# Cross-attention on one core: the first weight halves, the context and two block transposes are turned in another order

## The chip, the cores and the metric

The kernel runs on one core of a Trainium2 chip. Its engines are TensorE (PE in the profile, PEld for its weight loads), VectorE (DVE), ScalarE (ACT), GpSimd (POOL) and SyncE (SP), which here only issues transfers. The metric is the time of one execution on the device in microseconds; a lower time is better. Three executions of the kernel before took 283.97, 283.01 and 283.19 us, so its median is 283.19 us.

## The reference

One cross-attention layer with eight heads of width 256. There are 16 batches of 256 queries (width 256) and 77 keys (width 192), all in float32. The mask of the inputs is all ones.

```python
Q = (img_embed @ Wq).reshape(B, -1, H, D).transpose(0, 2, 1, 3)
K = (sent_embed @ Wk).reshape(B, -1, H, D).transpose(0, 2, 1, 3)
V = (sent_embed @ Wv).reshape(B, -1, H, D).transpose(0, 2, 1, 3)
score = jnp.einsum('bhqd,bhkd->bhqk', Q, K) / math.sqrt(D)
mask = (atten_mask != 0)[:, None, None, :]
score = jnp.where(mask, score, -jnp.inf)
attn = jax.nn.softmax(score, axis=-1)
ctx = jnp.einsum('bhqk,bhkd->bqhd', attn, V).reshape(B, -1, H * D)
out = ctx @ Wo + img_embed
mu = jnp.mean(out, axis=-1, keepdims=True)
var = jnp.var(out, axis=-1, keepdims=True)
return (out - mu) * jax.lax.rsqrt(var + EPS) * gamma + beta
```

## The kernel before

**What it computes.** The kernel never forms Q and K. For each head it multiplies the two weight matrices with each other once, G = Wk Wqᵀ / 16, and then multiplies the context c by G for a group of four batches: a = c G. Scores are then x aᵀ. Because the width of Wk is 192, G is kept in two pieces: `gA` (128 rows) and `gB` (the last 64 rows, two heads to a tile). The context is likewise kept turned, as `cA` and `cB`. In the same way Wv and Wo of a head are joined to one matrix (`uA`, `uB`).

**The opening stage.** To multiply Wk by Wq on TensorE both have to be turned, so that the head's width lies on the partitions. Half of the heads is turned on TensorE: `turn_q`, `turn_k`, `turn_k_last` and `turn_c` (for the context) each run four or six transposes into one or two PSUM banks, and copies then take the result to SBUF. The helper `evacuate` gives these copies in turn to ScalarE (line 151) and VectorE (line 153). The other half of the heads is turned by VectorE alone: `turn_blk(e)` (line 640) runs two stream transposes on blocks that were loaded as `wk_blk` and `wq_blk`. `keep_busy(n)` runs n transposes of the identity, whose results nobody reads.

**Order of the work.** The program writes each engine's order out by hand (a manual schedule): each engine does its instructions in the order of the lines. All loads are issued on SP, in the order of lines 567 to 594. In the diff's stretch, lines 751 to 766, the order on TensorE is: the first half of Wk's first 128 rows (`turn_k(0)`), Wk's last 64 rows for both halves (`turn_k_last`), the first half of Wq (`turn_q(0, 0)` and `turn_q(0, 1)`), their product (`g_of(0)`, line 719), the second half of Wk and of Wq, their product, the products for the last 64 rows (`rest_of_g`, line 733), and the first four batches' context (`turn_c(0, first)`, where `first` is 3). After this comes `a_of_places((0, 1))`, called A below: 64 matmul records at line 199 with `gA` (part A), 64 at line 213 with `gB` (part B), then eight copies to SBUF. Its eight outputs fill all eight PSUM banks. After A come the products for the heads that VectorE turned: `of_pair` (line 676, tile `pgb`) and `rest_of_pairs` (line 690, tile `phb`), A for the other places, the rest of the context, Wv times Wo (tiles `pu` and `pw`), and `prepare_last` (tile `pr`).

**The steady part.** From 58 us on a loop over the batches runs scores, softmax, the product with the values and the normalisation. PSUM tiles of all stages share one ring of eight banks, so a tile can be written when the copy of the tile eight places earlier is done.

Of the kernel before, what the change touches and what calls it, by code (L numbers as in the profile page):

```python
# [17 lines left out]
D = 256  # L18
# [35 lines left out]
def kernel(  # L54
# [13 lines left out]
    nc = tc.nc  # L68
# [67 lines left out]
    def flat(ap):  # L136
        return ap.rearrange("p a b -> p (a b)")
# [10 lines left out]
    def evacuate(dst, src):  # L148
        evacs[0] += 1
        if evacs[0] % 2:  # L150
            nc.scalar.copy(dst, src)  # L151
        else:
            nc.vector.tensor_copy(dst, src)  # L153
# [388 lines left out]
    with tc.tile_pool(name="wonce", bufs=1) as wp:  # L542
# [5 lines left out]
        wk_last = wp.tile([P, 2 * D], F32, tag="wl", name="wk_last")  # L548
# [8 lines left out]
        wk_ends = wk[P:].rearrange("r (e f) -> (r e) f", e=2)  # L557
# [5 lines left out]
        def load_c(lo, hi):  # L563
            nc.sync.dma_start(c_sb[:, lo:hi, :], c_rows[:, lo:hi, :])

        first = -(-GB * S2 // CR)
        nc.sync.dma_start(wk_nat[:, 0], wk_rows[0][:, : 2 * D])
        nc.sync.dma_start(wk_last, wk_ends[:, : 2 * D])
        nc.sync.dma_start(wq_nat[:, 0], wq_rows[0][:, :, : 2 * D])
        nc.sync.dma_start(wk_nat[:, 1], wk_rows[1][:, : 2 * D])  # L570
        nc.sync.dma_start(wq_nat[:, 1], wq_rows[1][:, :, : 2 * D])
        load_c(0, first)
        for e in range(2):
            load_blocks(wk_blk[:, e], wk_blocks[2 * e + 1])
# [24 lines left out]
        def keep_busy(n):  # L599
            for i in range(n):  # L600
                nc.tensor.transpose(idle, ident, ident)
# [9 lines left out]
        def turn_chunks(of, name):  # L611

            pt = ps_mm.tile([P, 4, P], F32, tag="mm", name=f"pt_{name}")
            for i, chunk in enumerate(of):
                nc.tensor.transpose(pt[:, i], chunk, ident)
            return pt

        def turn_q(e, u):
            chunks = [
                wq_nat[:, e, t, u * D + dc * P : u * D + (dc + 1) * P]  # L620
                for dc in range(2) for t in range(2)
            ]
            pt = turn_chunks(chunks, f"q_{e}_{u}")
            evacuate(flat(qT[:, e, u]), flat(pt))

        def turn_k(e):
            pt = turn_chunks([wk_nat[:, e, n * P : (n + 1) * P] for n in range(4)], f"k_{e}")
            evacuate(
                kT[:, e].rearrange("p u n l -> p (u n) l")[:, :, :P], pt
            )  # L630

        def turn_k_last():
            pt = turn_chunks([wk_last[:, n * P : (n + 1) * P] for n in range(4)], "kl")
            for e in range(2):
                evacuate(
                    kT[:, e].rearrange("p u n l -> p (u n) l")[:, :, P:],
                    pt.rearrange("p n (r e) -> p e n r", e=2)[:, e],
                )

        def turn_blk(e):  # L640
            for blk, of in ((wk_blk, kT_blk), (wq_blk, qT_blk)):
                nc.vector.transpose(
                    of[:, e].rearrange("p n (m r) -> p m n r", r=BK),
                    blk[:, e].rearrange("p m (n c) -> p m n c", c=BK),
                )

        def turn_c(lo, hi):
            for r in range(lo, hi, 2):
                n = min(2, hi - r)
                pc = ps_mm.tile([P, 4, P], F32, tag="mm", name=f"pc_{r}")  # L650
                for lc in range(2):
                    for j in range(n):
                        nc.tensor.transpose(
                            pc[:, 2 * lc + j, :CR],
                            c_sb[:, r + j, lc * LB : lc * LB + P],
                            ident[:CR, :CR],
                        )
                rows = slice(r * CR, (r + n) * CR)
                evacuate(flat(cA)[:, rows].rearrange("p (j m) -> p j m", m=CR), pc[:, :n, :CR])
                evacuate(  # L660
                    flat(cB)[LB:, rows].rearrange("p (j m) -> p j m", m=CR),
                    pc[LB:, 2 : 2 + n, :CR],
                )
                nc.gpsimd.tensor_copy(flat(cB)[:LB, rows], flat(cB)[LB:, rows])  # L664
# [34 lines left out]
        def two_banks(name, j):  # L699
            return [ps_mm.tile([P, 2, DI], F32, tag="mm", name=f"{name}_{j}_{e}") for e in range(2)]  # L700
# [13 lines left out]
        def g_of(e):  # L714

            pg = ps_mm.tile([P, 2, DI], F32, tag="mm", name=f"pg_{e}")
            for u in range(2):
                for dc in range(2):
                    nc.tensor.matmul(  # L719
                        pg[:, u],  # L720
                        kT[:, e, u, dc, :P],
                        qT[:, e, u, dc],
                        start=(dc == 0),
                        stop=(dc == 1),
                    )
            nc.scalar.mul(gA[:, NF * e : NF * e + 2], pg, D ** -0.5)

        def rest_of_g(u):

            ph = ps_mm.tile([P, DI], F32, tag="mm", name=f"ph_{u}")  # L730
            for dc in range(2):
                for e in range(2):
                    nc.tensor.matmul(
                        ph[half(e)],
                        kT[:, e, u, dc, P:],
                        qT[:, e, u, dc],
                        start=(dc == 0),
                        stop=(dc == 1),
                    )
            nc.vector.tensor_scalar(gB[:, u], ph, D ** -0.5, None, ALU.mult)  # L740

        def a_of_places(places, between=None):
            part_A, part_B, copies = prepare_a(0, places)
            part_A()
            part_B()
            for i, (dst, src) in enumerate(copies()):
                evacuate(dst, src)
                if between and i == 3:
                    between()

        turn_k(0)
        keep_busy(2)
        turn_k_last()
        keep_busy(3)
        turn_q(0, 0)
        turn_q(0, 1)
        g_of(0)
        turn_k(1)
        turn_q(1, 0)
        turn_q(1, 1)  # L760
        g_of(1)
        rest_of_g(0)
        rest_of_g(1)
        turn_c(0, first)
        turn_blk(0)
        a_of_places((0, 1), lambda: turn_blk(1))
        pg = two_banks("pgb", 0)
        for e in range(2):
            of_pair(pg, e, wk_part, wq_part)
# [7 lines left out]
        nc.sync.dma_start(gam, gamma.partition_broadcast(P))  # L777
        nc.sync.dma_start(bet, beta.partition_broadcast(P))
        a_of_places((2, 3))
        turn_v(3)  # L780
        turn_c(first, NCR)
# [167 lines left out]
```

## Time and profile before

| What | Value |
|---|---|
| Median of three executions | 283.19 us (283.01 to 283.97) |
| The profiled execution's own time | 282.59 us |
| Its span, first to last instruction | 280.8 us |
| TensorE busy | 270.8 us, 96% of the span |
| VectorE, ScalarE, GpSimd busy | 206.1, 166.5, 168.2 us |
| Transfers | 22.61 MB, mean 81 GB/s |
| Start of A's matmuls (line 199) | 17.27 us |
| First scores of the loop (line 313) | 58.25 us |

The profiled execution took 1.8 us more than its span; that is what lies around the first and the last instruction. All times in the text count from the span's start. A weight load or a matmul in float32 appears as more than one record, and a matmul's end is modelled, so a start is the better mark of time on TensorE. The time from a transfer's issue to its landing isn't that of the bytes alone: transfers queue behind each other.

### The profile page before, as it was taken

The numbers are of one execution on the slowest core, as the hardware profiler recorded it, in microseconds if no ns is written. First come the engines' busy times: TensorE is split into PE (matmuls) and PEld (weight loads), VectorE is DVE, ScalarE is ACT, GpSimd is POOL, SyncE is SP. The second block draws the span as 40 slices with busy tenths as digits, with TensorE's granted clock in tenths as the row PEclk, the third lists the DMA queues.
The fourth block names the chain that finished last, engine by engine and source line by source line (L and its number), as shares of the span: only waits on it lengthen the run. The fifth ranks groups of instructions, "written<-read, shape, count | busy, mean of one in ns | idle before, by whom it ended". The sixth has DMA issues, their size and how long they took to land.

```text
span 280.8 us, 13274 instructions
## 1 busy us (share of the span) xinstructions
PE 270.8 (96%) x5925; PEld 195.6 (70%) x5925; DVE 206.1 (73%) x421; ACT 166.5 (59%) x447; POOL 168.2 (60%) x228
## 2 busy tenths in 40 slices
PE   7899999999999999999999999999999999999990
PEld 7756589985586868686868686868686868476550
DVE  0255762668748989888889787777797978788873
ACT  2312142148547767676767676767686866968751
POOL 1000049955677777786867878777778445426173
PEclk9999999999999999999999999999999999999996
DMA  6998898940000010960100109501001011010112
GB/s 191 246 230 176 279 267 227 166 139 4 2 6 2 5 40 2 191 189 5 42 3 5 40 5 198 180 8 38 7 2 42 2 42 38 4 41 2 40 37 78
DMA packets 35641, 22.61 MB, mean 81 GB/s; under 512 B 17712, under 2 KB 34048, under 8 KB 35584
## 3 DMA queue, kind: packets, MB, share of 16 engines
q1 hardware_dynamic: 35584, 21.77, 30.8%
q8 instruction: 46, 0.75, 1.2%
q14 instruction: 11, 0.09, 0.1%
HBM read 17.57 MB, written 4.19 MB: 77 GB/s over the span
## 4 chain that ended last, share of the span: by engine, by line
PE 89%; POOL 2%; ACT 2%; DMA 2%; DVE 2%; issue 0%; SPq 0%; ACTq 0%; POOLq 0%
PE ps L313 23%; PE pa L199 12%; PE pv L241 9%; PE po L429 9%; PE pm L429 7%; PE pa L213 6%; PE pv L252 5%; PE po L378 5%; PE pu L676 3%; PE pr L274 2%; DMA wq_nat<-in_L_xattn_Wq_dram 2%; ACT e L342 1%; PE pg L719 1%; PE pgb L676 1%; PE pw L690 1%; PE pr L284 1%
## 5 line engine op out<-in xcount | busy, mean ns | idle before, releaser
L342 ACT ACTIVATE e<-s,top 128x77 f32<-128x77 f32 x256 | 67.1, 346 | 52.1 <-DVE top L335 49.9
L356 POOL TENSOR_TENSOR p<-e,rden 128x512 f32<-128x512 f32 x64 | 45.8, 738 | 46.6 <-DVE rden L350 46.4
L313 PE MATMUL ps<-a,xT 128*32 128x154 f32 x2048 | 70.0, 294 | 0.0
L313 PEld LDWEIGHTS ps<-a,xT 128*32 128x32 f32 x2048 | 66.2, 110 | 1.6 <-issue 0.7
L328 DVE TENSOR_TENSOR s<-ps,bias 128x308 f32<-128x308 f32 x64 | 30.3, 475 | 17.6 <-PE ps L313 15.9
L199 PE MATMUL pa<-cA,gA 128*32 128x308 f32 x512 | 35.8, 423 | 0.4 <-ACT cA L151 0.4
L462 POOL TENSOR_TENSOR xg<-xg,m 128x256 f32<-128x256 f32 x33 | 24.2, 733 | 13.5 <-DVE xg L476 11.8
L199 PEld LDWEIGHTS pa<-cA,gA 128*32 128x32 f32 x512 | 16.4, 110 | 21.1 <-issue 7.6
L241 PE MATMUL pv<-uA,cA 128*32 128x512 f32 x256 | 30.4, 592 | 0.0
L366 DVE STREAM_TRANSPOSE pT<-p 128x640 f32<-128x640 f32 x32 | 25.6, 824 | 2.4 <-POOL p L356 2.4
L348 DVE TENSOR_REDUCE den<-e 128x8 f32<-128x616 f32 x32 | 24.7, 772 | 3.5 <-ACT e L342 3.5
L335 DVE TENSOR_REDUCE top<-s 128x8 f32<-128x616 f32 x32 | 25.4, 795 | 1.1
L664 POOL COPY cB<-cB 64x224 f32<-64x224 f32 (+1 forms) x6 | 1.9, 358 | 36.8 <-DVE cB L153 36.8
L392 POOL TENSOR_TENSOR ts<-vw 128x768 f32<-128x768 f32 x11 | 22.0, 1997 | 0.0
L213 PE MATMUL pa<-cB,gB 64*32 64x308 f32 x512 | 19.5, 420 | 0.0
L378 PE MATMUL po<-vw,pT 128*32 128x256 f32 x320 | 19.2, 380 | 0.0
L861 ACT COPY vw<-pv 128x512 f32<-128x512 f32 x32 | 16.9, 578 | 2.5 <-PE pv L252 2.5
L495 ACT ACT_TABLE_LOAD x14 | 18.0, 1283 | 0.3
L213 PEld LDWEIGHTS pa<-cB,gB 64*32 64x32 f32 x512 | 9.7, 107 | 11.3 <-issue 7.6
L252 PE MATMUL pv<-uB,cB 64*32 64x512 f32 x256 | 17.4, 601 | 0.0
L524 DVE SCALAR_TENSOR_TENSOR xg<-xg,mv,gam 128x256 f32<-128x256 f32 x25 | 17.1, 682 | 0.0
L861 ACT COPY a<-pa 128x308 f32<-128x308 f32 x48 | 16.6, 446 | 0.0
(114 smaller groups left out, 440.1 us busy)
## 6 DMA issues: line engine op xcount, KB each, us to landing
xT<-in_x_dram SPq DMA_DIRECT2D x16, 256.0 KB, 6.4
xg<-in_x_dram SPq DMA_DIRECT2D x4, 1024.0 KB, 8.0
out_dram<-xg SPq DMA_DIRECT2D x15, 256.0 KB, 2.3
wo<-in_L_xattn_Wo_dram SPq DMA_DIRECT2D x4, 512.0 KB, 5.3
wvT<-in_L_xattn_Wv_dram SPq DMA_DIRECT2D x16, 96.0 KB, 3.7
wq_nat<-in_L_xattn_Wq_dram SPq DMA_DIRECT2D x2, 512.0 KB, 6.7
wq_blk<-in_L_xattn_Wq_dram SPq DMA_DIRECT2D x8, 128.0 KB, 4.3
wk_blk<-in_L_xattn_Wk_dram SPq DMA_DIRECT2D x8, 96.0 KB, 6.1
```

The source lines that it names most:

```text
L199: nc.tensor.matmul(flat(o[i * BK : (i + 1) * BK]), gA[:, h, cols(dc, i)], flat(cA[:, batches, :]), start=not B_first, stop=B_first,)
L213: nc.tensor.matmul(flat(banks[j + k][i * BK : (i + 1) * BK]), gB[half(k), h % NF, cols(dc, i)], flat(cB[half(k), batches, :]), start=B_fir ...
L241: nc.tensor.matmul(pv[k][i * BK : (i + 1) * BK], cA[:, b, k * BK : (k + 1) * BK], uA[:, parts, :, i], start=True, stop=False,)
L252: nc.tensor.matmul(pv[k][i * BK : (i + 1) * BK], cB[half(k), b, k * BK : (k + 1) * BK], uB[half(k), parts, :, i], start=False, stop=True,)
L313: nc.tensor.matmul(ps[m // 2][i * BK : (i + 1) * BK, m % 2 * 2 * S2 : (m % 2 + 1) * 2 * S2], xT_of[g][:, j * NM + m, dc], flat(a_of[g][:, ...
L328: nc.vector.tensor_tensor(s[:, a * H // 2 : (a + 1) * H // 2], ps[a][:, : H // 2 * S2].rearrange("p (h k) -> p h k", k=S2), bias[:, b, :]. ...
L342: nc.scalar.activation(e[:, h], s[:, h], AF.Exp, bias=top[:, h : h + 1])
L356: nc.gpsimd.tensor_tensor(part, e_mh[:, :, :, keys], rden_mh.unsqueeze(3).to_broadcast(list(part.shape)), ALU.mult,)
L366: nc.vector.transpose(pT_of[t].rearrange("p n m q -> p m n q"), p.rearrange("p m (n k) -> p m n k", k=BK),)
L378: nc.tensor.matmul(po[i * BK : (i + 1) * BK], pT[:, n, i], vw_of[b][:, 2 - n // 2 * 2 : 4 - n // 2 * 2, n % 2, :] if n < NF else vr[:, b, ...
L429: nc.tensor.matmul(out[i * BK : (i + 1) * BK], weight[:, i], moving, start=(n == 0), stop=(n == len(terms) - 1),)
L861: nc.scalar.copy(dst, src)
```

## The change

Four things move; no arithmetic is added or taken out, apart from one transpose of `keep_busy`.

- SP issues the load of Wk's last 64 rows (`wk_last`) after both halves of Wq and the second half of Wk, no longer ahead of them.
- `turn_k_last` moves behind `turn_q(1, 1)`, and the two `keep_busy` calls (2 and 3) become one of 4.
- `turn_k(1)` moves ahead of `g_of(0)`, and `turn_c(0, first)` moves ahead of `g_of(1)`.
- `turn_blk(1)`, which ran on VectorE after A's first four copies, moves ahead of A.

```diff
         nc.sync.dma_start(wk_nat[:, 0], wk_rows[0][:, : 2 * D])
-        nc.sync.dma_start(wk_last, wk_ends[:, : 2 * D])
         nc.sync.dma_start(wq_nat[:, 0], wq_rows[0][:, :, : 2 * D])
         nc.sync.dma_start(wk_nat[:, 1], wk_rows[1][:, : 2 * D])
         nc.sync.dma_start(wq_nat[:, 1], wq_rows[1][:, :, : 2 * D])
+        nc.sync.dma_start(wk_last, wk_ends[:, : 2 * D])
         load_c(0, first)
...
-        def a_of_places(places, between=None):
+        def a_of_places(places):
             part_A, part_B, copies = prepare_a(0, places)
             part_A()
             part_B()
-            for i, (dst, src) in enumerate(copies()):
+            for dst, src in copies():
                 evacuate(dst, src)
-                if between and i == 3:
-                    between()

         turn_k(0)
-        keep_busy(2)
-        turn_k_last()
-        keep_busy(3)
+        keep_busy(4)
         turn_q(0, 0)
         turn_q(0, 1)
+        turn_k(1)
         g_of(0)
-        turn_k(1)
         turn_q(1, 0)
         turn_q(1, 1)
+        turn_k_last()
+        turn_c(0, first)
         g_of(1)
         rest_of_g(0)
         rest_of_g(1)
-        turn_c(0, first)
         turn_blk(0)
-        a_of_places((0, 1), lambda: turn_blk(1))
+        turn_blk(1)
+        a_of_places((0, 1))
```

## The prediction

> **What bounds the kernel now.** I read the page's busy shares and chain first, to see whether an early gain can reach the end at all.
>
> ```profile
> PE 270.8 (96%) x5925; PEld 195.6 (70%) x5925; DVE 206.1 (73%) x421; ACT 166.5 (59%) x447; POOL 168.2 (60%) x228
> ...
> PE 89%; POOL 2%; ACT 2%; DMA 2%; DVE 2%; issue 0%; SPq 0%; ACTq 0%; POOLq 0%
> ```
>
> TensorE carries 89% of the chain. The DMA share (2%, the page names wq_nat) is one wait at the start; POOL's and most of ACT's and DVE's shares are the last 20 us. So whatever makes A start earlier moves the rest with it, unless a later transfer or copy is then too late. Next, the chain in order of time (start, duration, what):
>
> ```profile
> 1.62 5.56 DMA wq_nat<-in_L_xattn_Wq_dram
> 7.18 0.04 issue
> 7.23 0.67 PE pt_q L615 x4
> ...
> 7.92 0.70 DVE qT L153
> ...
> 8.76 1.97 PE pg L719 x8
> 10.72 0.44 PE pt_k L615 x4
> 11.16 0.45 PE pt_q L615 x4
> ...
> 11.63 0.59 ACT qT L151
> ...
> 12.27 1.99 PE pg L719 x8
> 14.27 1.88 PE ph L733 x16
> 16.14 0.55 PE pc L653 x4
> ...
> 17.27 4.35 PE pa L199 x64
> ```
>
> TensorE waits for the first half of Wq until 7.18, then three times for a copy: before the first pg, before the second, and before A. From 17.27 to 58 each piece of the chain is TensorE's. The third view is SP's issues in order of time, for the transfers:
>
> ```profile
> 3.08 0.47 SPq L564 DMA_DIRECT2D c_sb<-in_ctx_dram  x1
> ...
> 11.74 0.31 SPq L561 DMA_DIRECT2D wq_blk<-in_L_xattn_Wq_dram  x1
> ```
>
> The answers by tile give issue to landing: wk_nat 3.3 and 6.5 us, wk_last 3.6, wq_nat 5.6 and 7.9, c_sb 8.6. Added to the issue times (0.72, 2.10; 1.16; 1.62, 2.60; 3.08) the landings are 4.0 and 8.6; 4.8; 7.2 and 10.5; 11.7. The second line confirms the last: SP's list of waits has this stream of issues waiting for c_sb, and it goes on at 11.74, so c_sb was down at 11.72. Before, nobody noticed: turn_c ran at 16.07. The fourth view is the stretch round A's copies:
>
> ```profile
> 21.55 2.30 PE L213 MATMUL pa<-cB,gB 64*32 64x308 f32 x64
> 22.39 1.97 ACT L151 COPY a<-pa 128x308 f32<-128x308 f32 x4 [5.18 <-PE pa L213]
> 22.43 1.00 DVE L153 COPY a<-pa 128x308 f32<-128x308 f32 x2 [2.62 <-PE pa L213]
> ...
> 23.35 0.97 DVE L642 STREAM_TRANSPOSE kT_blk<-wk_blk 128x768 f32<-128x768 f32 x1
> 23.78 0.94 PEld L676 LDWEIGHTS pgb<-qT_blk,kT_blk 64*128 64x128 f32 x9 [0.50 <-ACT a L151]
> ...
> 24.24 1.20 DVE L642 STREAM_TRANSPOSE qT_blk<-wq_blk 128x1024 f32<-128x1024 f32 x1
> ...
> 25.36 0.83 DVE L153 COPY a<-pa 128x308 f32<-128x308 f32 x2
> ```
>
> VectorE idles 2.62 us before A's copies, and the second pair's transposes end at 25.44, just before the second half of pgb's 32 matmul records (23.78 + 3.96/2 = 25.8) reads them. TensorE doesn't stop there.
>
> **What the Trainium skill says.** "DMA: Bandwidth & Descriptors", section "Queues, rings and completion order": each DMA engine consumes descriptors in ring order. The landings above agree, in issue order. "PSUM — Partial Sum Buffer", section "Engine vs sequencer instructions": VectorE's queue is strict FIFO and matmuls start in program order, so one waiting instruction holds all behind it; here A's last two VectorE copies run at 25.36, behind the transposes. "TensorE: Matmul & The Clock Gate", Part 1: the clock is halved until one window of about 3.4 us was busy, and drops again after an idle one. The trace agrees with the first part: a transpose's weight load takes 230 ns up to 6.1 us (pt_kl) and 140 ns from 7.2 (pt_q). No gap here or below is near 3.4 us.
>
> **The load order.** 256 KB of wk_last go behind 1.25 MB. What SP issues from c_sb on is the same, with the same bytes ahead of it, so I leave c_sb at 11.72 and the blocks at their times; each issue from wk_blk's third waits for the landing of the transfer eight earlier, but the queue is never empty then (landings go on every 0.4 to 0.7 us). The total ahead at each landing before was 256 KB (4.0), 512 (4.8), 1024 (7.2), 1280 (8.6), 1792 (10.5). After: wq_nat's first half ends at 768 KB, half way between 4.8 and 7.2: about 6.0. wk_nat's second half ends at 1024 KB: 7.2. wq_nat's second ends at 1536, half way between 8.6 and 10.5: 9.5. wk_last: 10.5. These are estimates from the trace's landings. Bounds: from no move (7.2, 8.6, 10.5) to 5.6 for the first.
>
> **The transposes.** A transpose starts each 0.11 us at the full clock (0.44 for four) and 0.215 at half (four weight loads in 0.87). turn_k(0) ends near 5.24 and keep_busy(4) at 5.24 + 4 × 0.215 = 6.1; the removed fifth idle transpose and turn_k_last's 0.87 here cost nothing, since they filled a wait. turn_q: 6.1 to 7.1 (the first still slow). turn_k(1): from 7.23 for 0.44, to 7.67; during it the copies of Wq finish (DVE near 7.5, ACT near 7.8, the latter needed only half way through pg), so the wait before pg goes. pg: 1.97, to 9.64, 1.1 us earlier than now. turn_q: 0.89, to 10.53; turn_k_last: 0.44, to 10.98, on wk_last's 10.5. Then turn_c **waits for c_sb** until 11.72. This is a new wait; g_of(1), rest_of_g and all of A stand behind it on TensorE. It takes the place of the waits before the second pg and A.
>
> **From there to A.** 11.72 + 0.05 (landing to first transpose, as with wq_nat: 7.18 to 7.23) + 6 × 0.11 = 0.66 for turn_c + 1.99 (pg) + 1.88 (ph) = **16.30**. The copies of Wq, of wk_last and of the context all fit under these 3.9 us; gA's scaling (0.60) runs under ph, as now. A starts at 16.30 where it was 17.27: **0.97 us earlier**. The transposes' row alone would say 0.79 for turn_c with its modelled end, so the low value is 0.84.
>
> **The VectorE transposes.** turn_blk(0) follows gB's second scaling, near 16.3 + 0.45 = 16.75: 0.98 + 1.20 give 18.93. turn_blk(1): 0.97, to 19.9; its wq_blk lands at 15.74 + 4.3 = 20.04, then 1.20, to 21.3. A's first VectorE copy is due at 22.43 − 0.97 = 21.46. So the wait in VectorE's queue costs nothing, with 0.16 us to spare; even past this, pgb needs its second bank only when it starts, at 23.78 − 0.97 = 22.81, and the copy takes 0.5, so the block may land 20.04 + 1.0 before TensorE stops. Gain of that move: nothing, as TensorE did not wait there; the last VectorE copies come earlier (to 23.4), which nobody needs.
>
> **What is next late.** Moved 0.97 forward: pu at 36.8 needs Wo's first two blocks (29.52 + about 5, 34.5) and its second half, near 40.7, the last (30.47 + 7.6 = 38.1); Wv's blocks all are down by 31; x is down by 46.6 and turned at 51.89 − 0.97. The context's rest landed at 16.22 + 6.7 = 22.9 and is turned at 35.2. GpSimd's row from 38.79 starts from the context's copies and moves with them. So 0.97 stays to the end: span 279.8, that execution 281.6, and 283.19 − 0.97 = **282.2** for the median. The profiled execution lies 0.60 below the median, so the other executions have about that much which this trace doesn't show.
>
> **Rivals.** *Only the gaps count:* the landings don't move up, since the first bytes are slow for another reason. For it: wq_nat's 512 KB took 2.4 us after wk_last's 256 KB took 0.8. Then turn_q from 7.23 to 8.1, turn_k(1) waits until 8.6 and ends at 9.05, pg 11.0, turn_q 11.9, turn_k_last 12.35, turn_c 13.0, pg 15.0, ph 16.9: 0.37 us gained, 282.8. Against it: landings follow the ring's order.
>
> *More than forecast:* the clock is released later than the 6.3 us of this trace in other executions. The kernel before then pays up to 8 × 0.105 = 0.84 us for slow transposes after 7.2; the changed one has 0.74 us of slack before c_sb. Or c_sb lands sooner. With no wait for it A would start 0.74 earlier still. Gain 1.0 to 1.7: 281.5 to 282.1. For it: the executions differ by 0.96 us.
>
> *Slower:* the stream transpose of wq_blk is held by a late block and A's copies stand behind it. TensorE stops before pgb once the block lands after 21.0; the gain is eaten at 22.0, and 0.3% is lost at 22.9, when the time is 284.0. Against it: it would have to land 2.8 us later than its 20.04, with the same bytes ahead.
>
> **How the numbers follow.** 0.3% of 283.19 is 0.85 us, about what a measurement of this kernel can tell from no change, so the forecast is close to this line. Forecast: 0.60, with a scatter of some 0.4 us in c_sb's landing and the copies (281.8 to 282.6), 0.44 of it beyond the line and 0.16 within. More: 0.18. Only the gaps: 0.13. Slower: 0.06, and 0.03 for what I don't see. So faster 0.62, same 0.29, slower 0.09. The range 281.5 to 283.0 leaves out the slower cases and a tail of the others.
>
> **What would show it.** After: wq_nat's first half landing near 6.0; no wait before the first pg; a TensorE wait of about 0.7 us before pc, ended by c_sb, in place of the 0.4 before A; A at 16.3; VectorE's four stream transposes without a break from 16.8 to 21.3; A's copies at 21.4; everything from A to 58 in the same durations. I'm wrong if c_sb lands more than 0.3 us from 11.7, if A's start moves and the loop's first scores don't, or if pgb waits for a VectorE copy.

## The result and the profile after

Fifteen executions of each kernel: the changed kernel takes 281.44 us in the median (280.76 to 282.78), the kernel before 282.76 (282.11 to 283.97). The ratio over all executions is 0.9964, with a 95% interval of 0.9952 to 0.9976, which is about 1.0 us gained (0.7 to 1.4); the two medians alone differ by 1.3 us. The profiled execution took 280.93 us with a span of 279.2, where the kernel before had 282.59 and 280.8. It lies 0.5 us under the median of its kernel, so its gain is larger than the usual one.

The page of the changed kernel, its busy shares and its chain:

```profile
PE 269.7 (97%) x5924; PEld 194.8 (70%) x5924; DVE 206.0 (74%) x421; ACT 166.4 (60%) x447; POOL 168.2 (60%) x228
...
PE 88%; DMA 3%; POOL 2%; ACT 2%; DVE 1%; SPq 1%; issue 0%; ACTq 0%; POOLq 0%
```

The DMA share went from 2% to 3%, and the page now names c_sb for it. The chain in order of time (start, duration, what) says where it stands:

```profile
3.12 8.35 DMA c_sb<-in_ctx_dram
11.47 0.04 issue
11.51 0.80 PE pc L653 x6
12.31 1.74 PE pg L719 x8
14.05 1.88 PE ph L733 x16
15.93 4.29 PE pa L199 x64
20.21 2.23 PE pa L213 x64
22.45 3.65 PE pgb L676 x32
26.10 1.89 PE phb L690 x32
```

Nothing that TensorE does ahead of the context's landing (11.47) is in the chain any more, and from there to A there is no copy in it. The timeline shows the same head by TensorE's own starts (start, duration, instructions, then the wait and what ended it):

```profile
7.63 0.66 PE L615 MATMUL pt_k<-ident,wk_nat 128*128 128x128 f32 x4 [0.67 <-DMA wk_nat<-in_L_xattn_Wk_dram]
8.12 1.89 PE L719 MATMUL pg<-qT,kT 128*128 128x256 f32 x8
9.85 1.04 PE L615 MATMUL pt_q<-ident,wq_nat 128*128 128x128 f32 x8
10.73 0.60 PE L615 MATMUL pt_kl<-ident,wk_last 128*128 128x128 f32 x4
11.51 0.80 PE L653 MATMUL pc<-ident,c_sb 112*128 112x112 f32 x6 [0.18 <-DMA c_sb<-in_ctx_dram]
12.14 1.91 PE L719 MATMUL pg<-qT,kT 128*128 128x256 f32 x8
13.98 1.95 PE L733 MATMUL ph<-qT,kT 128*64 128x256 f32 x16
```

The three waits for copies are gone; a wait for the second half of Wk's rows and one for the context are there instead. (The printed 0.18 counts from the modelled end of the last transpose; from start to start 0.46 us passed where 0.11 would do.)

Three times tell where the span's 1.65 us come from. A starts at 15.86, before at 17.27: **1.41 us** (in two more profiles of this kernel, below, it starts at 16.66 and 16.65). From A's start to the loop's first scores it takes 40.75 us, before 40.99: **0.24 us**. From there to the end it takes 222.56 us in both. The 0.24 us lie in one place: from pgb's first start to phb's it takes 3.65 us (22.38 to 26.03), before 3.90 (23.78 to 27.68). That was not in the prediction.

### The profile page after: what moved, and what is told of

Read it like the earlier page. It is cut to its first block, busy times and chain, and to the rows that moved or that the text cites. A ratio compares the mean times of both kernels' runs of the same rounds, so it can differ in the third digit from the quotient of the medians.

```text
span 279.2 us, 13274 instructions
## 1 busy us (share of the span) xinstructions
PE 269.7 (97%) x5924; PEld 194.8 (70%) x5924; DVE 206.0 (74%) x421; ACT 166.4 (60%) x447; POOL 168.2 (60%) x228
## 4 chain that ended last, share of the span: by engine, by line
PE 88%; DMA 3%; POOL 2%; ACT 2%; DVE 1%; SPq 1%; issue 0%; ACTq 0%; POOLq 0%
PE ps L313 23%; PE pa L199 12%; PE pv L241 9%; PE po L429 9%; PE pm L429 7%; PE pa L213 6%; PE pv L252 5%; PE po L378 5%; DMA c_sb<-in_ctx_dram 3%; PE pu L676 3%; PE pr L274 2%; ACT e L342 1%; PE pw L690 1%; PE pgb L676 1%; PE pr L284 1%; PE pc L653 1%
## 5 line engine op out<-in xcount | busy, mean ns | idle before, releaser
L859 ACT COPY vw<-pv 128x512 f32<-128x512 f32 x32 | 16.9, 579 | 2.5 <-PE pv L252 2.5
L378 PEld LDWEIGHTS po<-vw,pT 128*32 128x32 f32 x320 | 10.0, 110 | 9.5 <-DVE den L348 2.5
```

The lines of the kernel that those rows point to most:

```text
L378: nc.tensor.matmul(po[i * BK : (i + 1) * BK], pT[:, n, i], vw_of[b][:, 2 - n // 2 * 2 : 4 - n // 2 * 2, n % 2, :] if n < NF else vr[:, b, ...
```

## The experiments

The head's time is counted below from one of two landings. In the *old order* A's start follows the landing of Wq's first half; in the *new order* it follows the landing of the context. Landings differ from one execution to the next, so A's start alone says little: the context's first rows landed between 11.13 and 12.27 in the eleven profiles that load them at this place.

**The second pair's transposes, alone and taken back.** First on the kernel before:

```diff
         turn_blk(0)
-        a_of_places((0, 1), lambda: turn_blk(1))
+        turn_blk(1)
+        a_of_places((0, 1))
```

> The kernel before with one part of the change alone: the second pair's stream transposes ahead of A. Theory of the prediction (TensorE did not stop there, so nothing is gained): ratio 1.000, A's start at 17.3, pgb's 32 records in 3.9 us as before. Rival (the transposes under pgb cost TensorE 0.25 us, by a weight load that stands waiting for them at the head of its queue): A's start unmoved, pgb in 3.7 us, ratio 0.9991, that is 0.25 us.

Measured: ratio 1.0002 (0.9991 to 1.0013). A starts at 16.91, 10.08 us after Wq's first half landed at 6.83; in the kernel before it is 10.09. pgb got no faster; it took 4.16 us, and TensorE's timeline shows a longer stop in it:

```profile
21.19 2.30 PE L213 MATMUL pa<-cB,gB 64*32 64x308 f32 x64
23.43 1.13 PE L676 MATMUL pgb<-qT_blk,kT_blk 64*128 64x256 f32 x8
24.80 2.86 PE L676 MATMUL pgb<-qT_blk,kT_blk 64*128 64x256 f32 x24 [0.24 <-issue]
27.59 0.66 PE L690 MATMUL phb<-qT_blk,kT_blk 64*64 64x256 f32 x8
```

The same edit taken back from the changed kernel:

> The changed kernel with the second pair's stream transposes back behind A's first four copies. Theory of the prediction: as the changed kernel, ratio 0.996 to 0.997 and pgb in 3.7 us. Rival (the weight load that waits for these transposes costs 0.25 us): A starts at 15.8 to 16.4 as in the changed kernel, pgb takes 3.9 us again, ratio about 0.001 above that of the changed kernel in the same call.

Measured: ratio 0.9947 (0.9933 to 0.9962), pgb 3.65 us. So the move of these transposes is worth nothing in either setting, and the weight load that waits for them is not what made pgb slow.

**The changed kernel twice more.**

> The changed kernel once more, beside the others. Theory (the prediction's chain: A starts some 4.4 us after the context's first rows land): A starts at 15.8 to 16.4 us, landing plus 4.4 within 0.15, ratio to before 0.995 to 0.997. From A's start to the loop's first scores it takes 40.75 us, as in the first profile of the changed kernel, where the kernel before took 40.98. Rival (the 0.25 us gained in pgb is chance): that stretch is 41.0 again.

> The changed kernel a third time, for a direct comparison with its parts on one chip. Theory (the start of A sets the gain): ratio 0.9955 to 0.9965, A 4.39 us after the context's landing, pgb 3.65 us.

Measured: ratios 0.9955 (0.9940 to 0.9971) and 0.9966 (0.9954 to 0.9978). A started at 16.66 and 16.65, later than forecast, and each time 4.39 us after the context's landing (12.27 and 12.26), as in the first profile (11.47 to 15.86). Both have pgb in 3.65 us, and 40.74 and 40.75 us from A to the first scores, so the 0.24 us are no chance.

**The load of Wk's last rows back in second place**, all else as in the changed kernel:

```diff
         nc.sync.dma_start(wk_nat[:, 0], wk_rows[0][:, : 2 * D])
+        nc.sync.dma_start(wk_last, wk_ends[:, : 2 * D])
         nc.sync.dma_start(wq_nat[:, 0], wq_rows[0][:, :, : 2 * D])
...
-        nc.sync.dma_start(wk_last, wk_ends[:, : 2 * D])
```

> The changed kernel with the load of Wk's last rows back in second place; the order on TensorE stays changed. Theory (landings follow the bytes ahead in the ring): Wq's first half lands at 7.0 to 7.3, Wk's second half at 8.4 to 8.7, the context still at 11.4 to 11.8; TensorE waits twice and reaches the context's transposes only near 13.0, so A starts at 16.6 to 16.9 and the ratio is 0.998 to 0.999. Rival (the load order is worth nothing, only the gaps filled by transposes count): A starts as in the changed kernel, near 16.0, ratio 0.996.

Measured: ratio 0.9968 (0.9952 to 0.9984). The landings went back as expected (7.05, 8.37, 10.45), but A didn't:

```profile
7.09 1.10 PE L615 MATMUL pt_q<-ident,wq_nat 128*128 128x128 f32 x8 [0.80 <-DMA wq_nat<-in_L_xattn_Wq_dram]
8.41 0.66 PE L615 MATMUL pt_k<-ident,wk_nat 128*128 128x128 f32 x4 [0.22 <-DMA wk_nat<-in_L_xattn_Wk_dram]
8.91 1.89 PE L719 MATMUL pg<-qT,kT 128*128 128x256 f32 x8
...
11.95 0.78 PE L653 MATMUL pc<-ident,c_sb 112*128 112x112 f32 x6
```

TensorE comes to the context at 11.95, 1.0 us earlier than I had worked out, and the context landed at 11.89. No wait is left there and none was needed: A starts at 16.28, again 4.39 us after the landing. Once the context's transposes are moved, the new load order only lets TensorE arrive early and wait. My expectation was wrong here (A at 16.6 to 16.9); the rival's was the nearer. The ratio's interval takes in both 0.996 and 0.998, so it is the trace that decides.

**The context's load later**, behind the first four blocks of Wk:

```diff
-        load_c(0, first)
         for e in range(2):
             load_blocks(wk_blk[:, e], wk_blocks[2 * e + 1])
+            if e == 0:
+                load_c(0, first)
```

> The changed kernel with the load of the context's first rows put behind the first four blocks of Wk (4 x 96 KB). Theory (the context's landing is on the path): it lands some 1.7 us later, near 13.2, A starts 4.39 us after the landing as in all runs of the new order, near 17.6, and the gain is gone: ratio 0.999 to 1.002. Rival (TensorE's own work sets A's start, the wait for the context has slack elsewhere): A starts at 16.0 to 16.7, ratio 0.996.

Measured: ratio 1.0078 (1.0043 to 1.0114), slower than the kernel before, where at most 1.002 was expected. The landing is at 14.46, not 13.2, since SP's issue of this load now stood at 6.32 behind a landing. A starts at 20.50, 6.04 us after it, where the changed kernel needs 4.39. TensorE's timeline, and the granted clock in stretches (columns: from and to, length, then busy time and count of PE, PEld, DVE, ACT and POOL, then clock, DMA share, GB/s):

```profile
11.25 0.63 PE L616 MATMUL pt_kl<-ident,wk_last 128*128 128x128 f32 x4 [0.22 <-DMA wk_last<-in_L_xattn_Wk_dram]
14.51 0.80 PE L654 MATMUL pc<-ident,c_sb 112*128 112x112 f32 x6 [2.63 <-DMA c_sb<-in_ctx_dram]
15.14 3.12 PE L720 MATMUL pg<-qT,kT 128*128 128x256 f32 x8
18.19 2.37 PE L734 MATMUL ph<-qT,kT 128*64 128x256 f32 x16
```

```profile
11.60:14.50 2.90, 0.28 (x3) 0.04 (x1) 0.58 (x2) 0.37 (x1) 0.00 (x0) 1.00 1.13 201
14.50:18.19 3.69, 3.68 (x14) 2.63 (x14) 0.58 (x2) 0.50 (x2) 0.59 (x2) 0.66 1.00 214
18.19:20.50 2.31, 2.31 (x18) 1.25 (x17) 0.42 (x1) 0.60 (x1) 0.00 (x0) 0.80 1.01 236
20.50:24.80 4.30, 4.30 (x70) 2.00 (x68) 4.18 (x5) 0.00 (x0) 0.00 (x0) 1.00 1.18 221
```

The landing is on the path: it is 2.99 us later than in the first profile of the changed kernel, and A is at least that much later. The other 1.6 us are the clock. After a wait of 2.63 us, and 1.2 us after its end, the clock fell to half (the trace's clock records have it from 15.68 to 19.09), and pg took 3.05 us from start to start in place of 1.84, ph 2.31 in place of 1.88.

The clock does not fall like this in every execution. Three of the seven (283.11, 283.31 and 284.46 us) have a mean granted clock of 0.995 or 0.996; with 3.41 us at half clock it could not be above 0.994. They are still 0.5 to 1.8 us above the kernel before's median of 282.64, so the late landing alone takes the gain away.

**The context's load earlier**, ahead of Wk's last rows, whose transposes then stand between g_of(1)'s two halves (its u loop gets a call after the first round):

```diff
+        load_c(0, first)
         nc.sync.dma_start(wk_last, wk_ends[:, : 2 * D])
-        load_c(0, first)
...
-        turn_k_last()
         turn_c(0, first)
-        g_of(1)
+        g_of(1, turn_k_last)
```

> The changed kernel with the context's first rows loaded ahead of Wk's last rows, their transposes before g_of(1), and those of Wk's last rows between g_of(1)'s two halves. Theory (the context's landing sets A's start, TensorE waits 0.4 us or more for it): the context lands near 10.5, TensorE comes to it at 10.6 to 10.8 and no longer waits, A starts at 15.5 to 15.8 in place of 15.9 to 16.7, ratio 0.993 to 0.995. Rival (Wk's last rows or the copies become the bound in its place): ph or the second half of pg waits, A starts near 16.2, ratio as the changed kernel's 0.996.

> The version with the context's rows loaded ahead of Wk's last rows, once more beside the changed kernel. Theory (it shortens the wait for the context to 0.2 us, and TensorE's own work becomes the bound): A at 15.7 to 16.1, 0.1 to 0.5 us ahead of the changed kernel, ratio 0.9945 to 0.9955 where the changed kernel has 0.9955 to 0.9965. Rival (no difference that can be measured): ratios within 0.0005.

Measured: 0.9945 (0.9928 to 0.9962) and 0.9953 (0.9936 to 0.9970). The context landed at 11.02 and 11.56, still behind TensorE, which waited 0.17 and 0.70 us. TensorE in the second of the two:

```profile
11.70 0.77 PE L653 MATMUL pc<-ident,c_sb 112*128 112x112 f32 x6 [0.70 <-DMA c_sb<-in_ctx_dram]
12.30 1.04 PE L719 MATMUL pg<-qT,kT 128*128 128x256 f32 x4
13.18 0.60 PE L615 MATMUL pt_kl<-ident,wk_last 128*128 128x128 f32 x4
13.61 1.03 PE L719 MATMUL pg<-qT,kT 128*128 128x256 f32 x4
14.57 2.06 PE L735 MATMUL ph<-qT,kT 128*64 128x256 f32 x16
16.57 4.36 PE L199 MATMUL pa<-cA,gA 128*32 128x308 f32 x64
```

A started at 16.03 and 16.57, 5.01 us after the landing in place of 4.39: 0.43 us of Wk's transposes now come after it, ph takes 0.12 us more, and the first transpose starts 0.1 us later after the landing. So A was not clearly earlier than in the changed kernel, and the start that I expected (15.5 to 15.8, then 15.7 to 16.1) did not come. Both ratios lie below those of the changed kernel, but their intervals overlap: not shown to be faster.

**One idle transpose more**, the changed kernel with keep_busy(5) in place of 4:

> The changed kernel with one idle transpose more, as many as in the kernel before. Theory (the 0.25 us in pgb hang on where in TensorE's stream of instructions a 16 KB fetch of instructions falls, which the number of idle transposes shifts): the fetch near 22 us is back, pgb takes 3.9 to 4.2 us, ratio about 0.001 above the changed kernel's. Rival (they hang on the new order, not on the count): the first fetch stays near 16 us and pgb takes 3.65 us, ratio as the changed kernel's, 0.9955 to 0.9965.

Measured: 0.9971 (0.9960 to 0.9983), pgb 3.65 us, the first fetch of instructions at 16.42. My expectation was wrong: one transpose more does not bring the slow pgb back.

**The context's transposes alone.** The kernel before, with nothing moved but this:

```diff
         turn_q(1, 1)
+        turn_c(0, first)
         g_of(1)
         rest_of_g(0)
         rest_of_g(1)
-        turn_c(0, first)
```

> The kernel before with one part alone: the context's first transposes ahead of g_of(1), loads and all else as before. Theory (the waits for copies before the second pg, 0.24, and before A, 0.40 with the 0.55 for the copy itself, are what the order removes): TensorE reaches the context after its landing, A starts at 16.3 to 16.8, ratio 0.998. Rival (most of the gain comes from the earlier landings and from turning Wk's second half in the first gap): A starts at 17.0 to 17.3, ratio 0.999 to 1.000.

> The kernel before with the context's first transposes ahead of g_of(1), once more. Theory (this one move carries the gain, as it takes the copies' waits before the second pg and before A away; the other moves only buy a wait for the context): the same ratio as the changed kernel in this call within 0.001, A near 16.6, pgb 3.65 us. Rival (the first result was luck in six runs, the other moves are worth 0.3 to 0.5 us): ratio 0.9975 to 0.998.

Measured: 0.9959 (0.9943 to 0.9976) and 0.9955 (0.9939 to 0.9971). This one move gives as much as the whole change. A started as expected (16.56 and 16.33), but the gain is about twice that of the expected 0.998; 0.24 us of the difference are pgb's, which the expectation left out. TensorE in the first of the two:

```profile
7.63 1.09 PE L615 MATMUL pt_q<-ident,wq_nat 128*128 128x128 f32 x8 [0.85 <-DMA wq_nat<-in_L_xattn_Wq_dram]
9.16 1.97 PE L719 MATMUL pg<-qT,kT 128*128 128x256 f32 x8 [0.44 <-DVE qT L153]
...
11.39 1.04 PE L615 MATMUL pt_q<-ident,wq_nat 128*128 128x128 f32 x8
12.27 0.74 PE L653 MATMUL pc<-ident,c_sb 112*128 112x112 f32 x6
12.85 1.91 PE L719 MATMUL pg<-qT,kT 128*128 128x256 f32 x8
14.68 1.95 PE L733 MATMUL ph<-qT,kT 128*64 128x256 f32 x16
16.56 0.72 PE L199 MATMUL pa<-cA,gA 128*32 128x308 f32 x8
```

The first copy's wait (0.44) is still there, those before the second pg and before A are not. From the landing of Wq's first half to A it takes 8.98 us in both profiles (7.58 to 16.56, 7.35 to 16.33), in the kernel before 10.09: 1.11 us, to which pgb adds 0.24. It needs no earlier landing: TensorE comes to the context at 12.27, which is after 11.63.

What the other moves give without this one was not run. An estimate from the starts of the changed kernel: with the context's transposes left behind the products for Wk's last rows, TensorE is done with `turn_k_last` at 11.16; then come 1.84 us for pg, 1.88 for ph, and 1.20 from the first of the context's transposes to A, as in the kernel before (16.07 to 17.27). That puts A at 16.1, where the whole change has 15.86 in this execution. So the other moves may bring A nearly as far forward by themselves; then the two ways do not add up. That only the context's move can carry the gain is not shown.

**The context's transposes between g_of(1) and rest_of_g**, again on the kernel before:

```diff
         g_of(1)
+        turn_c(0, first)
         rest_of_g(0)
         rest_of_g(1)
-        turn_c(0, first)
```

> The kernel before with the context's first transposes behind g_of(1) and ahead of rest_of_g: only the wait for the context's copy before A can go, the 0.24 us ahead of the second pg stays. Theory: no wait before A, A 0.3 to 0.5 us earlier against its own landing of Wq than in the kernel before (9.6 to 9.8 us after that landing, before 10.09), and, if the slow pgb hangs on TensorE waiting at A's first matmul, pgb in 3.65 us: ratio 0.9972 to 0.9982. Rival (the slow pgb hangs on the number of instructions ahead of A or on the second pg's wait): pgb 3.9 or more, ratio 0.998 to 0.999.

Measured: 0.9972 (0.9960 to 0.9984), A 9.47 us after Wq's landing (6.71 to 16.18), so 0.62 us less than before, and pgb in 3.65 us:

```profile
11.80 1.99 PE L719 MATMUL pg<-qT,kT 128*128 128x256 f32 x8 [0.24 <-ACT qT L151]
13.63 0.74 PE L653 MATMUL pc<-ident,c_sb 112*128 112x112 f32 x6
14.30 1.95 PE L733 MATMUL ph<-qT,kT 128*64 128x256 f32 x16
16.18 4.35 PE L199 MATMUL pa<-cA,gA 128*32 128x308 f32 x64
20.46 2.30 PE L213 MATMUL pa<-cB,gB 64*32 64x308 f32 x64
22.70 3.72 PE L676 MATMUL pgb<-qT_blk,kT_blk 64*128 64x256 f32 x32
```

The first step of the transposes, past rest_of_g, takes away the wait before A: 0.62 us of the head and the 0.24 us of pgb. The second step, past g_of(1), takes away the wait before the second pg and 0.49 us more.

## Why the prediction was right, and where its steps were not

The forecast was 0.97 us for the median, a ratio of 0.9966; 0.9964 was measured, and the time 281.44 lies just under the low end of the range for absolute times, 281.5, because the kernel before measured 282.76 over more executions, not 283.19 (0.9964 × 283.19 would be 282.2). That the size came so close is in part luck. In the three profiles of the changed kernel the context landed at 12.00 on average, 0.28 us later than forecast; the way from there to A was 0.19 us shorter than the sum; and the 0.24 us in pgb stand in no term of it. Taken point by point:

- **What bounds A: right.** The context's landing sets A's start in all three profiles of the changed kernel, and a later landing moves A back. Predicted start 16.30; measured 15.86, 16.66 and 16.65, on average 16.39. The landing scatters by more than the 0.4 us that I had allowed (11.47 to 12.27). A landing more than 0.3 us from 11.7 was to be a sign of being wrong; two of the three profiles show it, and the gain stayed.
- **From the landing to A: right, a term mis-sized.** The sum was 0.05 + 0.66 + 1.99 + 1.88 = 4.58; it measured 4.39. The term is pg's 1.99. From start to start it is 1.93 in the kernel before (12.27 to 14.20), since the row's length includes the modelled end; and 0.09 of that is the slower first start after a wait, so that behind running transposes it is 1.84.
- **The load order: right in its landings, wrong in its worth.** Landings of 6.0, 7.2, 9.5 and 10.5 were estimated; 5.7, 7.6, 9.4 and 10.5 came. TensorE waited 0.67 us for Wk's second half, which was not forecast and cost only slack. But with the old load order A starts at 16.28. The step that failed is in the rival *only the gaps*: its 16.9 has 1.95 and 2.0 for the two pg (1.73 and 1.83 in the run) and a landing of 8.6 for Wk's second half (8.37); with these put right it is the forecast itself. So, once the context's transposes are moved, this part of the change, and with it the moves of Wk's last rows and of Wk's second half, buys only slack ahead of the context; moving the context's transposes alone is as good.
- **The second pair's transposes: nothing, as predicted, but not by the path described.** I had the last block down at 20.04 and 0.16 us to spare. The block landed later, and VectorE's queue stood. ScalarE's and VectorE's rows of the changed kernel:

```profile
20.98 1.97 ACT L151 COPY a<-pa 128x308 f32<-128x308 f32 x4 [6.30 <-PE pa L213]
20.99 1.25 DVE L642 STREAM_TRANSPOSE qT_blk<-wq_blk 128x1024 f32<-128x1024 f32 x1 [1.72 <-DMA wq_blk<-in_L_xattn_Wq_dram]
22.16 1.60 DVE L153 COPY a<-pa 128x308 f32<-128x308 f32 x4
22.37 3.32 PEld L676 LDWEIGHTS pgb<-qT_blk,kT_blk 64*128 64x128 f32 x32 [0.50 <-ACT a L151]
```

  The issue of that block to its landing took 5.4 us (15.43 to 20.86). VectorE waited 1.72 us with A's copies behind the transpose, as the rival *slower* describes, and began them 1.2 us after ScalarE. The break that the prediction ruled out (four stream transposes from 16.8 to 21.3 without one) was there. It cost nothing, because pgb did not need VectorE. The prediction, from the kernel before, had pgb's second bank wait for VectorE's first copy; in the changed kernel the waits of pgb's first two weight loads both name ScalarE's copies, of which two had ended by 21.93. So its second bank was not that of A's second output, eight tiles earlier, which VectorE copies. VectorE's first copy ended only at 22.60, after pgb's start at 22.38, and that start comes 0.35 us after the last of part B in both kernels. With A at 15.86 the point from which that rival decides would be 20.6 in place of 21.0; the block landed after it, and TensorE did not stop. That point was put too early.
- **The rest of the chain: right.** 222.56 us from the first scores to the end in both; no later transfer was missed.
- **Missing: the 0.24 us in pgb.** I had read that TensorE does not stop there. Between 24.54 and 24.89 it started nothing, where a pair of matmuls starts every 0.215. The matmuls' one row of 3.96 us for all 32 records hid this, but the weight loads of the kernel before break there, at a wait that the trace gives no cause for:

```profile
24.89 2.46 PEld L676 LDWEIGHTS pgb<-qT_blk,kT_blk 64*128 64x128 f32 x23 [0.17 <-issue]
```

## What to carry to other kernels

Where one engine carries the chain, list its waits for copies and ask for each which work that is ready, and wanted later, can be put between a producer and its consumer: here six transposes, moved past two groups of matmuls, took away two waits and gave as much as the whole change. Once the gaps were filled, the next landing was the bound, and earlier landings of everything ahead of it bought only slack; put the sum together from landings on, and try each part of a change alone before keeping it. Take durations from start to start in a running stretch, not from a row that begins with a wait.

## What the runs showed of the hardware that was not expected

- **The clock fell after less than a window.** The Trainium skill ("TensorE: Matmul & The Clock Gate", Part 1) lets the clock drop after an idle window of about 3.4 us, and the prediction took every gap below this as safe. With the context's load late a wait of 2.63 us was enough for 3.41 us at half clock, which cost 1.6 us. The prediction's claim held only because its own gaps stayed short: in the other thirteen profiles no wait of TensorE in the opening stage after 3 us is longer than 1.16 us. In all fourteen profiles the stretches between two changes of the clock are whole multiples of 3.413 us; in this run they are 10.24, 3.41 and 262.83 us, so 3, 1 and 77 of them. If the windows lie on that grid, the one that ended at 15.68 had begun at 12.27, and TensorE was idle in 2.2 of its 3.4 us (until 14.51). This is an estimate from one profile; how long a wait is safe was not measured.
- **Where pgb was slow, a fetch of instructions came late.** The trace's instruction queue moves 16 KB at a time. In the two profiles with a slow pgb (3.90 us in the kernel before, 4.16 with the second pair's transposes moved alone) the first fetch after the start of the program came 4.7 and 5.2 us after A's start; in the eleven others with no long wait for the context and pgb at 3.65 us it came between 0.4 us ahead of A's start and 0.7 us after it, and in the run with the late context, pgb 3.65 us too, 2.5 us after. The slow ones are those whose first matmul of A had to wait for a copy, and moving the context's transposes took both away, as was expected of their first step. In both slow profiles TensorE stops at the same place, after eight of pgb's 32 records. But the fetch had ended by 23.46 in both, 1.1 and 0.7 us before the stop began. That the late fetch makes TensorE stop there was not tried by itself, and the cause stays open.
